# A convolution and a column recurrence on one core: the first stage moves into the blocks' buffers, and the matrices in memory get 112 rows

## The chip, the cores and the metric

The kernel runs on one core of a Trainium2 chip. A core has five engines with a queue of instructions each: PE (TensorE, matrix products; its weight loads are listed apart as PEld), ACT (ScalarE), DVE (VectorE), POOL (GpSimd) and SP (SyncE, which here only issues transfers). Sixteen DMA engines move data between the chip's memory (HBM) and the core's buffers (SBUF, 128 partitions); PE writes to PSUM. Engines wait for each other and for transfers by semaphores. The metric is the device time of one execution in microseconds (us). Before the change three runs took 5189.91, 5190.26 and 5219.42 us; the median is 5190.26.

## The reference

The input `x` has 4 images of 64 channels, 256 x 256 pixels, float32. Two layers are computed, each on a group norm of its input and added to it:

```python
x = x + _L0_conv_ref(_gn(x), ...)   # layer 0
x = x + _L1_conv_ref(_gn(x), ...)   # layer 1

def _L0_conv_ref(x, w1, w_dw, w_out, ln_w, ln_b):
    hidden = einsum('bchw,oc->bohw', x, w1)            # 64 -> 384 channels, pointwise
    hidden = depthwise 3x3 convolution of hidden, padding SAME
    q, k, v = split(hidden, 3, axis=1)                 # 128 channels each
    out = irfft2(rfft2(patches8x8(q)) * rfft2(patches8x8(k)))
    out = layer norm of out over the channels
    return einsum('bchw,oc->bohw', v * out, w_out)     # 128 -> 64 channels
```

`_gn` is a group norm with 32 groups of 2 channels, so every image needs its mean and variance before anything of it can be convolved. Layer 1 is a gated recurrent cell (`_gru_cell`) that walks over the 256 columns of the image; a column takes the column before it, shifted by -1, 0 and +1 rows, as its state.

## The kernel before, in words

The program has three parts in order of time.

**The first stage** (lines 211 to 274) does two things at once. It builds the matrices of layer 0: a depthwise 3x3 convolution followed by the transform of an 8x8 patch is, per channel, one product of the 10x10 window (`HALO = 100` values) with a 100 x 64 matrix. `bt` (the constants of the nine taps) and `wd` (the weights) are multiplied on PE in 32 steps into PSUM (`banks`), ACT copies each step into `ts`, and three transfers on POOL's queue (`keep_matrices`) write `ts` to memory as `t_all`, of shape [3, 100, 8, 1024]: kind 0 for q, 1 for k, 2 for v, 100 rows of 8 groups of 16 channels. Beside this, `seen_piece` loads image 0 in 16 pieces of 1 MB through SP into five rotating buffers (`xc`), and DVE takes their statistics (`bn_stats`); after the last piece `norm_of_pieces` (line 83) turns them into the scale and shift of image 0 (`sc0`). The windows of the first block, `xq`, four transfers of 800 KB, come on POOL's queue behind the three `t_all` writes. The stage has pools of its own (`xa`, `sta`, `bps`), which are given back at its end.

**Layer 0** (lines 276 to 709) handles 32 blocks of 32 image rows one after the other. `normalize` applies the group norm to `xq`. Then PE makes `h`, the pointwise product, for one third of the channels at a time (three chunks of 16 units; `pointwise`), and after each chunk multiplies `h` by the matrices: `transform` for q and k (`circular` takes their product and `inverse` transforms it back into `z`), `values` for v. The layer norm (`layer_norm`), the gate and the projection of a block run beside the next block's products. The matrices do not stay in SBUF: `fetch` brings them anew for each block, 24 transfers of 16 channels, each [100 rows, 1024 values], 400 KB, through SP into four rotating tiles `t` (line 326). A fetch is issued four matrices ahead, and waits until PE has finished with the matrix that was in its tile. `wk` holds the work space of q and k, `seen` the piece of the next image whose statistics are taken in passing (`look`, `count`), on POOL's queue.

**Layer 1** (lines 716 to 900) goes over the 256 columns.

The order on each engine is that in which the program is written: every instruction goes through `InOrder`, which keeps it. Waits are derived from the tiles that instructions read and write. SP's queue is used by the pieces, the constants, the fetches and the residual loads (`residual`); POOL's by `t_all`, `xq`, `look` and the stores of layer 0's result (`leave`); ACT's by the taps and weights. An instruction that waits holds up everything behind it on its queue.

Of the kernel before, what the change touches and what calls it, by code (L numbers as in the profile page):

```python
# [9 lines left out]
F32 = mybir.dt.float32  # L10
# [6 lines left out]
HID = 6 * C  # L17
# [7 lines left out]

NBLK = B * W // 32
HALO = 100
NJ = 64
NP = 2 * NJ

# [52 lines left out]
def norm_of_pieces(nc, st, t, psum, eps, sc):  # L83

    m_all, d, total, mean = t[:, 256:264], t[:, 264:272], t[:, 272:273], t[:, 273:275]
    nc.vector.tensor_copy(m_all, st[:, :, 0])
    nc.vector.tensor_reduce(total, m_all, mybir.AxisListType.X, ALU.add)
    yield  # L90
    pm = psum()
    for i in range(2):
        nc.tensor.matmul(pm[:, i : i + 1], lhsT=t[:, P * i : P * i + P], rhs=total, start=True, stop=True)
    nc.vector.tensor_copy(mean, pm)
    nc.vector.tensor_tensor(d, m_all, mean[:, 0:1].to_broadcast([P, 8]), ALU.subtract)
    nc.vector.tensor_tensor(d, d, d, ALU.mult)
    nc.vector.tensor_tensor(d, d, st[:, :, 1], ALU.add)
    nc.vector.tensor_reduce(total, d, mybir.AxisListType.X, ALU.add)
    yield
    pv = psum()[:, 0:1]  # L100
    nc.tensor.matmul(pv, lhsT=t[:, P : 2 * P], rhs=total, start=True, stop=True)
    nc.scalar.activation(sc[:, 1:2], pv, AF.Sqrt, bias=eps, scale=1.0)
    nc.vector.reciprocal(sc[:, 1:2], sc[:, 1:2])
    nc.vector.scalar_tensor_tensor(sc[:, 0:1], mean[:, 1:2], -1.0, sc[:, 1:2], ALU.mult, ALU.mult)
    yield
# [57 lines left out]
def tile_conv_then_gru(  # L163
# [21 lines left out]
    x1 = dram.tile([B, C, W, H], F32, tag="x1", name="x1")  # L185


    t_all = dram.tile([3, HALO, 8, 16 * NS], F32, tag="t_all", name="t_all")


    layer0 = ExitStack()
    xp = layer0.enter_context(tc.tile_pool(name="xp", bufs=4))
    xq = {}

    def load(n, jq):

        t = xp.tile([P, 16, HALO], F32, tag="xq", name=f"xq_{n}_{jq}")
        nc.gpsimd.dma_start(t, xh[n, :, 16 * jq : 16 * jq + 16, :])
        xq[n, jq] = t

    def piece(of, b, i, w, n):

        w0 = i * (W // 16) + w
        return of[b].rearrange("c (a w) h -> (c a) w h", a=2)[:, w0 : w0 + n, :].rearrange("p w h -> p (w h)")
# [3 lines left out]
    sc0 = const.tile([P, B, 2], F32, tag="sc0", name="sc0")  # L208
    st0 = const.tile([P, 8, 2], F32, tag="st0", name="st0")
    bn0 = const.tile([P, 8, 6], F32, tag="bn0", name="bn0")  # L210
    with tc.tile_pool(name="xa", bufs=5) as xa, tc.tile_pool(name="sta", bufs=1) as sta, tc.tile_pool(
        name="bps", bufs=1, space=PSUM
    ) as bps:
        bt = sta.tile([P, 32, HALO], F32, tag="bt", name="bt")
        wd = sta.tile([P, HID], F32, tag="wd", name="wd")
        for i in range(4):
            nc.scalar.dma_start(wd[32 * i : 32 * i + 9], w_dw)
            nc.scalar.dma_start(bt[32 * i : 32 * i + 9], taps[i])
        eps = const.tile([P, 1], F32, tag="eps", name="eps")
        nc.gpsimd.memset(eps, EPS)  # L220
        ts = sta.tile([HALO, 3 * P, NS], F32, tag="ts", name="ts")
        banks = bps.tile([P, 8, 512], F32, tag="b", name="psb")

        def keep_matrices(i):
            nc.gpsimd.dma_start(
                t_all[i].rearrange("p n k -> p (n k)"),
                ts[:, i * P : (i + 1) * P].rearrange("p c k -> p (c k)"),
            )

        for i in range(32):  # L230
            kind, s = i // 16, i % 16
            c0, num = 2 * P * kind, 2 * P - P * kind
            ps = banks[0:HALO, 4 * (i % 2) : 4 * (i % 2) + 4, 0:num]
            for k in range(4):
                at = slice(32 * k, 32 * k + 9)
                nc.tensor.matmul(
                    ps[:, k],
                    lhsT=bt[at, i, :],
                    rhs=wd[at, c0 : c0 + num],
                    start=True,  # L240
                    stop=True,
                    tile_position=(32 * k, 0),
                )
            nc.scalar.copy(ts[:, c0 : c0 + num, 4 * s : 4 * s + 4], ps.rearrange("p s c -> p c s"))
            if i == 15:
                keep_matrices(0)
                keep_matrices(1)
        keep_matrices(2)
        for jq in range(4):
            load(0, jq)  # L250
        def seen_piece(i):
            xc = xa.tile([P, 2048], F32, tag="xc", name=f"xc_{i}")
            nc.sync.dma_start(xc, piece(x, 0, i // 2, i % 2 * 8, 8))
            for k in range(4):
                nc.vector.bn_stats(bn0[:, i % 2 * 4 + k, :], xc[:, 512 * k : 512 * k + 512])
            if i % 2:
                nc.vector.bn_aggr(st0[:, i // 2, :], bn0)

        for i in range(6):
            seen_piece(i)  # L260
        avg = sta.tile([P, 512], F32, tag="avg", name="avg")
        nc.sync.dma_start(avg[:, 0 : 2 * P].rearrange("p (a q) -> p a q", a=2), sums)
        w1_sb = const.tile([P, HID], F32, tag="w1", name="w1_sb")
        nc.sync.dma_start(w1_sb, w1.rearrange("a c o -> (a c) o"))
        g_sb = const.tile([P, 2, 2, NS], F32, tag="g", name="g_sb")
        nc.sync.dma_start(g_sb, g12.rearrange("a s r n p -> (a s) r n p"))
        wo_sb = const.tile([P, 4, C], F32, tag="wo", name="wo_sb")
        nc.sync.dma_start(wo_sb, w_out.rearrange("a f b c -> (a f) b c"))
        ln_sb = const.tile([P, 2, 4], F32, tag="ln", name="ln_sb")
        nc.sync.dma_start(ln_sb, ln.rearrange("a f n b -> (a f) n b"))  # L270
        for i in range(6, 16):
            seen_piece(i)
        for _ in norm_of_pieces(nc, st0, avg, lambda: banks[:, 0:2, 0], eps, sc0[:, 0]):
            pass
    st1 = const.tile([P, NBLK, 2], F32, tag="st1", name="st1")
    with layer0 as s:
        big = s.enter_context(tc.tile_pool(name="big", bufs=1))
# [8 lines left out]
            place[0] = (at + banks) % 8  # L286
            return ring[:, at % 8 : at % 8 + banks]

        h = big.tile([HALO, P, NP], F32, tag="h", name="h")
        z = big.tile([P, NJ, E], F32, tag="z", name="z")  # L290
        v = big.tile([P, NJ, E], F32, tag="v", name="v")
        wk = big.tile([P, 7, 1024], F32, tag="wk", name="wk")
        lnst = big.tile([P, 512], F32, tag="lnst", name="lnst")
        seen = big.tile([P, 1024], F32, tag="seen", name="seen")
        moments = big.tile([P, 2, NJ], F32, tag="moments", name="moments")
        def normalize(n, jq):

            t, b, at = xq[n, jq], n // 8, n % 8
            flat = t.rearrange("p j k -> p (j k)")
            shift, rstd = sc0[:, b, 0:1], sc0[:, b, 1:2]  # L300
            if jq == 3:
                nc.vector.tensor_scalar(flat, flat, rstd, shift, ALU.mult, ALU.add)
            else:
                nc.scalar.activation(flat, flat, AF.Identity, bias=shift, scale=rstd)
            grid = t.rearrange("p j (r c) -> p j r c", c=10)
            if jq % 2 == 0:
                nc.gpsimd.memset(grid[:, 0, :, 0:1], 0.0)
            else:
                nc.gpsimd.memset(grid[:, 15, :, 9:10], 0.0)
            if at == 0 and jq < 2:  # L310
                nc.gpsimd.memset(grid[0:C, :, 0, :], 0.0)
            if at == 7 and jq >= 2:
                nc.gpsimd.memset(grid[C:P, :, 9, :], 0.0)
# [8 lines left out]
        def fetch(count):  # L322
            while len(streamed) < min(count, NBLK * 24):
                m, r = divmod(len(streamed), 24)
                t = tp.tile([P, 16, NS], F32, tag="t", name=f"t_{m}_{r}")
                nc.sync.dma_start(t[0:HALO].rearrange("p c k -> p (c k)"), t_all[order[r][0], :, order[r][1]])
                streamed.append(t)
                matrices[m, order[r]] = t

# [270 lines left out]
        def go(steps=1):  # L600
            for _ in range(steps):
                if norm:
                    next(norm, None)

        for n in range(NBLK + 1):
# [14 lines left out]
            for unit in range(16):  # L620
                if unit < 14:
                    pointwise(n, 0, unit, unit in (3, 9) if norm else unit % 2)
                elif unit == 14:
                    last_two = [unit_of(n, 0, unit, False)]
                else:
                    last_two.append(unit_of(n, 0, unit, False))
                    for span in ((0, 16), (16, P)):
                        for copy in last_two:
                            copy(*span)
                if unit in (0, 3, 6, 9, 12):  # L630
                    go()

            def beside_first(sp):
                if n and sp < 3:
# [326 lines left out]
```

## Time and profile before

One execution was profiled: its own time is 5200.96 us, and its span, from the first to the last instruction, is 5199.2 us.

| what | value |
|---|---|
| median of three runs | 5190.26 us |
| profiled execution, span | 5200.96 us, 5199.2 us |
| first stage, up to the first pointwise matmul | 102.8 us |
| layer 0, 32 blocks | from there to about 3760 us |
| busy PE, DVE, ACT, POOL | 4911.1, 4038.0, 3348.7, 1724.5 us |
| fetches of matrices | 768 of 400 KB |
| writes of the matrices | 3 of 3200 KB, landing after 19.8, 31.5 and 34.7 us |
| moved by DMA in all | 784.55 MB, mean 151 GB/s |

How to read the answers of the profile: a row of the timeline has the start (us), the busy time of a run of like instructions (us), the engine, the line in the kernel, the operation, output and input, and in brackets how long the engine had been idle and what ended that. Nearly all instructions have line 157, that of `InOrder`, so tiles tell them apart. The row of a group has its count, then the sum and the mean (ns) of its busy time, then the idle time just before its instructions, by releaser. "issue" is idle time for which the profile shows no releaser. DMA share is the mean share of the time in which the sixteen DMA engines had a packet in hand.

### The profile page before, as it was taken

Reading aid. Unit: us, or ns where it says so; the run is one execution under the profiler, and the core shown is the slowest. Engines: PE = TensorE matmul, PEld = TensorE weight load, DVE = VectorE, ACT = ScalarE, POOL = GpSimd, SP = SyncE. Lnnn points to the kernel's source line nnn. Section 1 sums busy time; section 2 is a strip of 40 time slices with the busy share of each in tenths; the row PEclk is TensorE's granted clock in tenths of the full one; section 3 lists DMA queues with packets and bytes.
Section 4 is the critical chain, followed back from the end, with each engine's and each line's share of the span. In section 5 each row is a group of like instructions: output and inputs, shape, how many; then the busy total and the mean of one; then the engine's idle time right before and its main releaser. Section 6 shows DMA issues by size and latency. Waiting matters only on the chain.

```text
span 5199.2 us, 275863 instructions
## 1 busy us (share of the span) xinstructions
PE 4911.1 (94%) x127092; PEld 4202.2 (81%) x127092; DVE 4038.0 (78%) x7000; ACT 3348.7 (64%) x4253; POOL 1724.5 (33%) x1723
## 2 busy tenths in 40 slices
PE   4999999999999999999999999999789999999999
PEld 3887888788888888888887888888578888888888
DVE  4678888877888887788887777878667777777777
ACT  3666667666666766666666666667466666666665
POOL 0233333333333333333333323223333333333333
PEclk9999999999999999999999999999899999999999
DMA  7566665666666666666656656655443333333332
GB/s 266 148 171 178 185 180 166 168 175 169 171 188 173 171 170 175 172 178 180 186 160 162 151 155 164 168 159 151 111 123 99 100 98 99 100 100 100 97 100 71
DMA packets 421174, 784.55 MB, mean 151 GB/s; under 512 B 32604, under 2 KB 295552, under 8 KB 417632
## 3 DMA queue, kind: packets, MB, share of 16 engines
q1 hardware_dynamic: 366464, 533.76, 38.1%
q0 software_dynamic: 53264, 232.55, 15.3%
q8 instruction: 997, 16.33, 1.4%
q14 instruction: 161, 1.32, 0.1%
q10 hardware_dynamic: 288, 0.58, 0.0%
HBM read 622.72 MB, written 144.05 MB: 147 GB/s over the span
## 4 chain that ended last, share of the span: by engine, by line
PE 78%; DVE 7%; issue 5%; ACT 5%; DMA 4%; POOL 1%; ACTq 0%; POOLq 0%; SPq 0%; DVEq 0%
PE psring L157 57%; PE pshz L157 7%; PE pshr L157 6%; PE psni L157 5%; PE pshn L157 3%; DMA t<-t_all 2%; ACT z L157 2%; DVE n L157 2%; ACT v L157 1%; DVE wk L157 1%; ACT xq L157 1%; DVE st L157 1%; DVE g L157 1%; DVE z L157 1%; DMA wk<-in_sums 1%
## 5 line engine op out<-in xcount | busy, mean ns | idle before, releaser
L157 PEld LDWEIGHTS psring<-h,t 100*32 100x32 f32 x49152 | 1383.5, 119 | 249.1 <-issue 195.7
L157 PE MATMUL psring<-h,t 100*32 100x128 f32 x49152 | 1464.3, 257 | 96.7 <-issue 59.0
L157 PEld LDWEIGHTS psring<-w_sb,xq 64*100 64x100 f32 x24576 | 1372.6, 164 | 123.1 <-issue 89.7
L157 PE MATMUL psring<-w_sb,xq 64*100 64x128 f32 x24576 | 1430.4, 273 | 34.2 <-issue 21.6
L157 ACT COPY h<-psring 100x1024 f32<-100x1024 f32 (+2 forms) x1371 | 1234.1, 988 | 336.8 <-PE psring L157 335.9
L157 DVE TENSOR_TENSOR wk<-psring,wk 128x1024 f32<-128x1024 f32 (+1 forms) x768 | 759.5, 1037 | 461.5 <-PE psring L157 320.2
L157 POOL TENSOR_TENSOR v<-v,z 128x2048 f32<-128x2048 f32 x128 | 582.7, 4557 | 658.6 <-DVE wk L157 603.0
L157 DVE TENSOR_TENSOR z<-z,moments 128x2048 f32<-128x2048 f32 x256 | 578.0, 2279 | 2.3
L157 POOL TENSOR_TENSOR wk<-wk 128x1024 f32<-128x1024 f32 x128 | 303.4, 2371 | 618.7 <-DVE wk L157 596.6
L157 POOL TENSOR_TENSOR raw<-raw,st 128x512 f32<-128x512 f32 x256 | 303.1, 1184 | 530.6 <-DVE st L157 471.5
L157 ACT COPY z<-psring 128x2048 f32<-128x2048 f32 x128 | 238.9, 1866 | 348.8 <-PE psring L157 248.2
L157 PE MATMUL pshr<-st,wi 64*64 64x144 f32 (+7 forms) x12240 | 429.7, 269 | 6.7 <-DVE st L157 6.7
L157 DVE COPY h<-psring 100x1024 f32<-100x1024 f32 x229 | 277.5, 1214 | 198.7 <-PE psring L157 192.7
L157 PE MATMUL psni<-st,wi 64*64 64x144 f32 (+7 forms) x12240 | 428.6, 269 | 1.3 <-issue 1.3
L157 PE MATMUL pshz<-st,wi 64*64 64x144 f32 (+7 forms) x12240 | 428.8, 269 | 0.1
L157 ACT ACTIVATE z<-pshz,b_rz 128x288 f32<-128x288 f32 (+7 forms) x510 | 242.0, 475 | 281.3 <-PE pshz L157 275.8
L157 ACT COPY wk<-psring 128x1024 f32<-128x1024 f32 x256 | 259.5, 1014 | 249.5 <-PE psring L157 214.4
L157 DVE BATCH_NORM_STATS2 lnst<-z 128x6 f32<-128x128 f32 x2048 | 416.8, 282 | 0.0
L157 ACT COPY v<-psring 128x2048 f32<-128x2048 f32 (+1 forms) x160 | 243.3, 1521 | 251.0 <-PE psring L157 251.0
L157 PEld LDWEIGHTS pshr<-st,wi 64*64 64x64 f32 x12240 | 370.0, 133 | 41.1 <-DVE st L157 9.8
L157 PEld LDWEIGHTS psni<-st,wi 64*64 64x64 f32 x12240 | 369.7, 133 | 31.3 <-issue 0.7
L157 PE MATMUL psring<-wk,g_sb 32*64 32x512 f32 x6144 | 382.1, 600 | 9.2 <-issue 5.9
(96 smaller groups left out, 6170.2 us busy)
## 6 DMA issues: line engine op xcount, KB each, us to landing
t<-t_all SPq DMA_DIRECT2D x768, 400.0 KB
xq<-in_xh POOLq DMA_DIRECT2D x128, 800.0 KB, 6.1
wk<-in_x SPq DMA_DIRECT2D x256, 256.0 KB
x<-wk POOLq DMA_DIRECT2D x256, 256.0 KB, 5.4
seen<-in_x POOLq DMA_DIRECT2D x96, 512.0 KB, 7.6
raw<-x SPq DMA_DIRECT2D x128, 256.0 KB
raw<-x SPq DMA_DIRECT2D x256, 128.0 KB
out<-raw SPq DMA_DIRECT2D x128, 256.0 KB
```

Of the source, the lines that this page charges most:

```text
L157: return self.tc.keep_in_program_order(got(*args, **kwargs))
```

## The change

The first stage no longer has buffers of its own. `h`, `z`, `v` and `wk` of layer 0 are allocated first, and the stage borrows them: the image pieces, `bt`, `wd` and `avg` lie in `h` (`hx`), the matrices of kind 0 in `wk`, of kind 1 in `z`, of kind 2 in `v`; `seen` becomes an eighth slice of `wk`. The matrices go to memory later: kinds 0 and 1 on SP's queue after the last image piece, in three transfers, kind 2 on POOL's queue in the first block, after the sixteenth unit of its first chunk. `xq` of block 0 comes on SP's queue, between the pieces, and the weights `wd` on POOL's. ACT copies a step of kinds 0 and 1 in two instructions instead of one, and applies a Sqrt to one column before the norm. The stage computes with `ring`, the PSUM tile of layer 0.

In memory `t_all` has `ROWS = 112` rows instead of 100, and every fetch brings 112. The last twelve are zeros (cleared by one memset on DVE and two on POOL, from row 96 on); PE reads 100 as before.

```diff
 HALO = 100
+ROWS = 112
...
-    t_all = dram.tile([3, HALO, 8, 16 * NS], F32, tag="t_all", name="t_all")
+    t_all = dram.tile([3, ROWS, 8, 16 * NS], F32, tag="t_all", name="t_all")
...
-    def load(n, jq):
+    def load(n, jq, queue=nc.gpsimd):
...
-        nc.gpsimd.dma_start(t, xh[n, :, 16 * jq : 16 * jq + 16, :])
+        queue.dma_start(t, xh[n, :, 16 * jq : 16 * jq + 16, :])
...
+        hx = big.tile([P, P * NP], F32, tag="h", name="h")
+        h = hx[0:HALO].rearrange("p (c n) -> p c n", n=NP)
...
+        wk = big.tile([P, 8, 1024], F32, tag="wk", name="wk")
+        seen = wk[:, 7]
...
+        bt = hx[:, 10240:13440].rearrange("p (i k) -> p i k", k=HALO)
+        wd = hx[:, 13440 : 13440 + HID]
+        avg = hx[:, 13824 : 13824 + 512]
+        ts = (
+            wk[0:ROWS].rearrange("p a (c k) -> p (a c) k", k=NS),
+            z[0:ROWS].rearrange("p n e -> p (n e)").rearrange("p (c k) -> p c k", k=NS),
+            v[0:ROWS].rearrange("p n e -> p (n e)").rearrange("p (c k) -> p c k", k=NS),
+        )
         for i in range(4):
-            nc.scalar.dma_start(wd[32 * i : 32 * i + 9], w_dw)
             nc.scalar.dma_start(bt[32 * i : 32 * i + 9], taps[i])
+            nc.gpsimd.dma_start(wd[32 * i : 32 * i + 9], w_dw)
...
+        nc.vector.memset(wk[96:ROWS], 0.0)
+        for t in (z, v):
+            nc.gpsimd.memset(t[96:ROWS], 0.0)
+
+        def keep_matrices(queue, i, k0, k1):
+            queue.dma_start(
+                t_all[i, :, k0:k1].rearrange("p n k -> p (n k)"),
+                ts[i][:, 16 * k0 : 16 * k1].rearrange("p c k -> p (c k)"),
             )
...
-            nc.scalar.copy(ts[:, c0 : c0 + num, 4 * s : 4 * s + 4], ps.rearrange("p s c -> p c s"))
-            if i == 15:
-                keep_matrices(0)
-                keep_matrices(1)
-        keep_matrices(2)
-        for jq in range(4):
-            load(0, jq)
+            for part in range(2 - kind):
+                nc.scalar.copy(
+                    ts[2 * kind + part][0:HALO, :, 4 * s : 4 * s + 4],
+                    ps[:, :, P * part : P * part + P].rearrange("p s c -> p c s"),
+                )
+
+        for i in range(32):
+            matrices_of(i)
+        nc.scalar.activation(moments[:, 0, 0:1], eps, AF.Sqrt, bias=eps, scale=1.0)
+
         def seen_piece(i):
-            xc = xa.tile([P, 2048], F32, tag="xc", name=f"xc_{i}")
+            xc = hx[:, 2048 * (i % 5) : 2048 * (i % 5) + 2048]
...
-        for i in range(6):
+        for i in range(10):
             seen_piece(i)
+            if i in (4, 6, 8):
+                load(0, i // 2 - 2, nc.sync)
...
-        for i in range(6, 16):
+        for i in range(10, 16):
             seen_piece(i)
-        for _ in norm_of_pieces(nc, st0, avg, lambda: banks[:, 0:2, 0], eps, sc0[:, 0]):
+            if i == 10:
+                load(0, 3, nc.sync)
+        for i, k0, k1 in ((0, 0, 8), (1, 0, 4), (1, 4, 8)):
+            keep_matrices(nc.sync, i, k0, k1)
+        for _ in norm_of_pieces(nc, st0, avg, lambda: ring[:, 0:2, 0], eps, sc0[:, 0]):
             pass
...
-                nc.sync.dma_start(t[0:HALO].rearrange("p c k -> p (c k)"), t_all[order[r][0], :, order[r][1]])
+                nc.sync.dma_start(t[0:ROWS].rearrange("p c k -> p (c k)"), t_all[order[r][0], :, order[r][1]])
...
                 if unit in (0, 3, 6, 9, 12):
                     go()
+                if n == 0 and unit == 15:
+                    keep_matrices(nc.gpsimd, 2, 0, 8)
```

More of the change, by code (lines that the diff above doesn't have):

```diff
@@ L210, in tile_conv_then_gru @@
     bn0 = const.tile([P, 8, 6], F32, tag="bn0", name="bn0")
[L211 to L216, printed above, removed]
-            nc.scalar.dma_start(wd[32 * i : 32 * i + 9], w_dw)
[L218 to L243, printed above, removed]
-            nc.scalar.copy(ts[:, c0 : c0 + num, 4 * s : 4 * s + 4], ps.rearrange("p s c -> p c s"))
-            if i == 15:
-                keep_matrices(0)
-                keep_matrices(1)
-        keep_matrices(2)
-        for jq in range(4):
-            load(0, jq)
-        def seen_piece(i):
-            xc = xa.tile([P, 2048], F32, tag="xc", name=f"xc_{i}")
[L253 to L257, printed above, removed]
-        for i in range(6):
[L260 to L270, printed above, removed]
-        for i in range(6, 16):
-            seen_piece(i)
-        for _ in norm_of_pieces(nc, st0, avg, lambda: banks[:, 0:2, 0], eps, sc0[:, 0]):
-            pass
@@ L275, in tile_conv_then_gru @@
+    st1 = const.tile([P, NBLK, 2], F32, tag="st1", name="st1")
     st1 = const.tile([P, NBLK, 2], F32, tag="st1", name="st1")
@@ L287, in psum @@
             return ring[:, at % 8 : at % 8 + banks]
-        h = big.tile([HALO, P, NP], F32, tag="h", name="h")
+        hx = big.tile([P, P * NP], F32, tag="h", name="h")
+        h = hx[0:HALO].rearrange("p (c n) -> p c n", n=NP)
         z = big.tile([P, NJ, E], F32, tag="z", name="z")
         v = big.tile([P, NJ, E], F32, tag="v", name="v")
-        wk = big.tile([P, 7, 1024], F32, tag="wk", name="wk")
+        wk = big.tile([P, 8, 1024], F32, tag="wk", name="wk")
+        seen = wk[:, 7]
@@ L293, in tile_conv_then_gru @@
         lnst = big.tile([P, 512], F32, tag="lnst", name="lnst")
-        seen = big.tile([P, 1024], F32, tag="seen", name="seen")
         moments = big.tile([P, 2, NJ], F32, tag="moments", name="moments")
+        bt = hx[:, 10240:13440].rearrange("p (i k) -> p i k", k=HALO)
[6 more added lines that the diff above has]
+        )
@@ new lines, in tile_conv_then_gru @@
+        for i in range(4):
+            nc.scalar.dma_start(bt[32 * i : 32 * i + 9], taps[i])
+            nc.gpsimd.dma_start(wd[32 * i : 32 * i + 9], w_dw)
+        eps = const.tile([P, 1], F32, tag="eps", name="eps")
+        nc.gpsimd.memset(eps, EPS)
+        nc.vector.memset(wk[96:ROWS], 0.0)
[6 more added lines that the diff above has]
+            )
@@ new lines, in matrices_of @@
+        def matrices_of(i):
+            kind, s = i // 16, i % 16
+            c0, num = 2 * P * kind, 2 * P - P * kind
+            ps = ring[0:HALO, 4 * (i % 2) : 4 * (i % 2) + 4, 0:num]
+            for k in range(4):
+                at = slice(32 * k, 32 * k + 9)
+                nc.tensor.matmul(
+                    ps[:, k],
+                    lhsT=bt[at, i, :],
+                    rhs=wd[at, c0 : c0 + num],
+                    start=True,
+                    stop=True,
+                    tile_position=(32 * k, 0),
+                )
+            for part in range(2 - kind):
+                nc.scalar.copy(
+                    ts[2 * kind + part][0:HALO, :, 4 * s : 4 * s + 4],
+                    ps[:, :, P * part : P * part + P].rearrange("p s c -> p c s"),
+                )
@@ new lines, in tile_conv_then_gru, with seen_piece @@
+        for i in range(32):
+            matrices_of(i)
+        nc.scalar.activation(moments[:, 0, 0:1], eps, AF.Sqrt, bias=eps, scale=1.0)
+        def seen_piece(i):
+            xc = hx[:, 2048 * (i % 5) : 2048 * (i % 5) + 2048]
+            nc.sync.dma_start(xc, piece(x, 0, i // 2, i % 2 * 8, 8))
+            for k in range(4):
+                nc.vector.bn_stats(bn0[:, i % 2 * 4 + k, :], xc[:, 512 * k : 512 * k + 512])
+            if i % 2:
+                nc.vector.bn_aggr(st0[:, i // 2, :], bn0)
@@ new lines, in tile_conv_then_gru @@
+        for i in range(10):
+            seen_piece(i)
+            if i in (4, 6, 8):
+                load(0, i // 2 - 2, nc.sync)
+        nc.sync.dma_start(avg[:, 0 : 2 * P].rearrange("p (a q) -> p a q", a=2), sums)
+        w1_sb = const.tile([P, HID], F32, tag="w1", name="w1_sb")
+        nc.sync.dma_start(w1_sb, w1.rearrange("a c o -> (a c) o"))
+        g_sb = const.tile([P, 2, 2, NS], F32, tag="g", name="g_sb")
+        nc.sync.dma_start(g_sb, g12.rearrange("a s r n p -> (a s) r n p"))
@@ new lines, in tile_conv_then_gru @@
+        wo_sb = const.tile([P, 4, C], F32, tag="wo", name="wo_sb")
+        nc.sync.dma_start(wo_sb, w_out.rearrange("a f b c -> (a f) b c"))
+        ln_sb = const.tile([P, 2, 4], F32, tag="ln", name="ln_sb")
+        nc.sync.dma_start(ln_sb, ln.rearrange("a f n b -> (a f) n b"))
+        for i in range(10, 16):
+            seen_piece(i)
+            if i == 10:
+                load(0, 3, nc.sync)
+        for i, k0, k1 in ((0, 0, 8), (1, 0, 4), (1, 4, 8)):
+            keep_matrices(nc.sync, i, k0, k1)
@@ L296, in normalize @@
+        for _ in norm_of_pieces(nc, st0, avg, lambda: ring[:, 0:2, 0], eps, sc0[:, 0]):
+            pass
         def normalize(n, jq):
```

## The prediction

> **What bounds the kernel now.** I read the page first, for who is busiest. PE has 94% of the span, and in the page's chain of work that ended last it holds 78%. So time is won only where PE stands still; everything else is cover.
>
> ```profile
> PE 4911.1 (94%) x127092; PEld 4202.2 (81%) x127092; DVE 4038.0 (78%) x7000; ACT 3348.7 (64%) x4253; POOL 1724.5 (33%) x1723
> ...
> q8 instruction: 997, 16.33, 1.4%
> ```
>
> The second line is the queue that brings the program itself: 997 packets for 16.33 MB, so 16 KB a packet. Over 275,863 instructions that is 59 bytes each; as some records can be missing I take 64, and 256 instructions a packet.
>
> Then I asked who made PE wait, longest first in total (us, times, longest):
>
> ```profile
> PE psring L157 <- issue: 87.9, 95, 3.1
> ...
> PE psring L157 <- DMA t<-t_all: 15.3, 27, 1.6
> ```
>
> "issue" means that nothing in the profile was waited for. I laid these gaps beside the trace's records of the instruction queue: 95 of the layer's gaps end within 0.35 us of the end of a 16 KB packet on it. So they are PE out of instructions. After such a landing the next packet starts 2.6 us later at the earliest and takes about 1.05 us, 3.7 us in all; and 256 instructions are 128 matmuls with their weight loads, which in the transforms (320 matmuls in 8.99 us) last 3.6 us. There PE eats its program as fast as it can arrive, so whatever delays a packet stops PE. Of the 87.9 us, 59.0 lie ahead of the matmuls that read the matrices (row of the groups: idle before, by releaser):
>
> ```profile
> L157 PE MATMUL psring<-h,t 100*32 100x128 f32 x49152 | 1464.3, 257 | 96.7 <-issue 59.0 <-DMA t<-t_all 14.4 <-ACT h L157 13.1
> ```
>
> Last, the first stage, which ends at 102.77 us. Its stretches of 10 us (busy us of PE, PEld, DVE, ACT, POOL; clock; DMA share; GB/s):
>
> ```profile
> 0.00:10.00 10.00, 1.14 (x2) 0.40 (x2) 2.47 (x4) 0.00 (x0) 0.30 (x5) 1.00 0.87 230
> 10.00:20.00 10.00, 2.32 (x8) 0.88 (x8) 5.32 (x9) 1.28 (x1) 0.00 (x0) 1.00 0.99 257
> 20.00:30.00 10.00, 9.10 (x66) 3.91 (x66) 8.06 (x14) 7.68 (x8) 0.00 (x0) 1.00 0.89 336
> 30.00:40.00 10.00, 8.98 (x80) 3.89 (x76) 7.55 (x13) 8.27 (x10) 0.38 (x1) 1.00 1.01 423
> 40.00:50.00 10.00, 8.94 (x116) 5.77 (x112) 7.67 (x14) 7.85 (x14) 0.91 (x2) 1.00 1.04 405
> 50.00:60.00 10.00, 0.38 (x8) 0.04 (x4) 1.33 (x4) 0.71 (x2) 2.70 (x5) 1.00 1.01 384
> 60.00:70.00 10.00, 0.00 (x0) 0.00 (x0) 1.79 (x4) 0.00 (x0) 0.00 (x0) 1.00 0.94 366
> 70.00:80.00 10.00, 0.00 (x0) 0.00 (x0) 2.84 (x5) 0.00 (x0) 0.00 (x0) 1.00 0.91 341
> 80.00:90.00 10.00, 0.00 (x0) 0.00 (x0) 2.47 (x4) 0.00 (x0) 0.00 (x0) 1.00 0.82 293
> ```
>
> From 50 us on all engines stand and the DMA runs full: the stage is as long as the bytes ahead of its last image piece. These rows hold 30.4 MB by 90 us. The page's DMA list gives what went: image pieces 16 x 1024 KB = 16.8 MB, xq 4 x 800 KB = 3.3, constants 1.1, and t_all 3 x 3200 KB = 9.8; together 31.0. The timeline shows the pieces held back behind t_all, then the end of the stage:
>
> ```profile
> 47.80 2.47 DVE L157 BATCH_NORM_STATS2 bn<-xc 128x6 f32<-128x512 f32 x4 [2.26 <-DMA xc<-in_x]
> ...
> 92.40 2.47 DVE L157 BATCH_NORM_STATS2 bn<-xc 128x6 f32<-128x512 f32 x4 [3.09 <-DMA xc<-in_x]
> ...
> 98.56 1.28 ACT L157 ACT_TABLE_LOAD   x1 [47.52 <-PE psb L157]
> ...
> 102.77 16.56 PEld L157 LDWEIGHTS psring<-w_sb,xq 64*100 64x100 f32 x256 [4.39 <-POOL xq L157]
> ```
>
> **The first stage.** *Moved:* t_all's writes now stand behind the last piece on SP's queue. Ahead of the piece are 16.8 + 3.3 + 1.1 = 21.2 MB. By the rows 16.5 MB have moved at 50 us; the other 4.7 at 384 GB/s take 12.2, so it lands at 62. From the last landing to the first matmul it is 102.77 - 92.40 = 10.4 us; the Sqrt table, now loaded early, takes 1.28 off that: 71. I add 2 us for pieces waiting for one of five buffers, as now: 73, **30 us earlier**.
>
> *Added, hidden:* ACT's 16 copies of 1024 elements (1.01 us) become 32 of 512 (0.57 us by the row of that size), 2 us more; they end near 53 instead of 51, before 62. DVE clears 16x8192 of wk first: by its TENSOR_SCALAR of 1600 elements (1.11 us) 5.7 us, by its COPY of 1024 (1.23 us) 9.8; then 16 pieces of 2.84 us end by 56, before 62. POOL clears z and v: two memsets of xq (10 and 160 elements, 0.12 and 0.24 us) give 6.6 us each, the 2048-element multiply (4.56 us) 18; z is ready by 10 to 21, v by 17 to 40, first written by ACT at about 21 and 42. With that cover gone each of these would push ACT by its own length, and the piece at 62 still ends later.
>
> *Late next:* t_all. wk and z hold 2 x 3.67 MB on SP; at 375 GB/s (the rows of 50 to 70) they end at 82, the first four matrices (1.8 MB) at 87. They are needed 17 us after the first matmul, at 90. But POOL adds an image look (0.5 MB, waiting for wk's write, with v's write queued behind it; POOL's next work, the first crossed add, is 27 us behind the first matmul now) and v's 3.67 MB from about 78, and between 50 and 70 POOL's queue visibly took more than SP's. If all 4.2 MB go first, the matrices come at 98, 8 us late; if none, not late. I take 4: **-26 us**. Ends: -30, and -10 if HBM takes the writes at about half pace (then 16 more are lost). z's first write, 14 us after the transforms begin, and v's, 80 after, come behind the writes that read them.
>
> **The fetches.** 768 fetches now carry 112 rows. A packet of a row takes 159 ns in most records. Where only matrices move, the records show ten packets in flight at 614 of 1,178 sampled moments, over eleven at 9: 100 rows use ten DMA engines of sixteen. The 128-row pieces fill sixteen (share 1.01 above), the 9-row taps go as nine packets each. I infer that rows are split evenly over the most engines that divide them: 112 = 16 x 7. Ends: ten engines as for 100 rows, sixteen as for 128; I take sixteen. Then an engine gets 7 packets, 1.1 us, in place of 10, 1.6 us. In a transform a matrix is used up in 1.87 us, so ten engines are 85% full with t alone, sixteen 60%. The 37.7 MB more (768 x 49 KB) take 2.6% of sixteen engines over the layer, mean DMA share 0.62: no cost while it stays below full. SP issues the same 768.
>
> The Trainium skill, page "DMA: Bandwidth & Descriptors", section "Why a DMA increments its semaphore by 16 and not by 1", states the same split and names 100 partitions as ten engines; by it 112 are sixteen. If it were ten, both terms below would be nothing.
>
> What waits on them: the chain of waits runs over a fetch some two dozen times, as here (start, us, what), issue to landing 5.4 to 6.9 us:
>
> ```profile
> 123.68 5.61 DMA t<-t_all
> 129.29 0.14 issue
> 129.42 31.94 PE psring L157 x782
> ```
>
> Four buffers leave a fetch three matrices' time, 3 x 1.87 = 5.6 us. With 0.5 us less work and no standing queue it fits: of 15.3 us I take **-13** (ends 0 and -15).
>
> **The program's own packets** share these engines. In stretches where nothing but t had moved in the 4 us before, the records show 52 gaps (47 us) ahead of h,t and 7 (5 us) ahead of g_sb. After a landing the next packet starts at 2.6 to 2.8 us in about a third of the cases and at 3 to 8 in the rest, also beside t alone, as if some packets met t's queue and some did not. Sixteen less full engines should halve these 52 us: **-25**. Ends: -52, and a loss (below). The 22 us ahead of the pointwise matmuls come beside xq loads and stay.
>
> **Sum:** -26 - 13 - 25 = -64 us. The profiled execution took 5200.96 us (span 5199.2 and 1.8 around it): 5137. It lies 10.7 above the median of the three runs, 5190.26, so the median becomes **5126 us**, 1.2% faster. 1%, 52 us, is about what a measurement of this kernel can tell from no change.
>
> **Rivals.**
> - *The packets of the program do not care* (0.20). For it: 2.6 us of their 3.7 is a fixed delay. Against: long delays occur beside t alone. Then 5190 - 39 = **5151**.
> - A rule in the Trainium skill would make it so: "Runtime: NRT & Kernel Launch", section "Instruction fetch mechanics", calls the cost of crossing a 16 KiB block mostly hidden; the 95 gaps that end on such a packet speak against it here.
> - *The change does not do what it says* (0.10): 112 rows stay on few engines, and only the stage gains: **5164**.
> - *The stage gives back its gain* (0.11): t_all lands late, -10 in place of -26: **5142**.
> - *Slower* (0.07): the program's packets lie on the six engines that t leaves free today, and t now covers all sixteen. The h,t matmuls are 98,304 instructions, 384 packets, of which some 62 end a gap today, 0.94 us each. If a third of the other 322 get one, that is +101; with -26 and -13, +62: **5252**. It decides for "slower by 1%" from about 97 new gaps (91 us). Against: the 52 gaps beside t alone, which free engines would not have.
>
> **Numbers.** The forecast has 0.52. Its own spread is about 5100 to 5150, below 5138 in three of four; with a third of the late stage and a fifth of the first rival that makes 0.47 for faster by over 1%, 0.07 for slower, 0.46 between. The range goes from 5098 (-30, -15, -47) to 5172 (past the stage-only case, with some of its loss) and leaves out the slower rival and the far ends.
>
> **What would show it.** The first pointwise matmul near 73 us and the first transform by 90 to 95; the chain no longer over t; PE's wait for t under 3 us; more packets of t in flight than ten; "issue" on psring near 60 us. Wrong if "issue" grows, if the transforms of the first image wait past 98, or if the last image piece is not at 62.

## The result, and the profile after

The changed kernel took 5150.57 us (median of 6 runs, 5141.58 to 5159.27), the kernel before on the same chip 5199.66 (6 runs, 5189.91 to 5219.42): a ratio of 0.9902, 95% interval 0.9881 to 0.9923, so 1.0% faster. The forecast was 5126 of 5190, a ratio of 0.9876. The profiled execution of after took 5159.27 us, its span is 5157.5, 41.7 less than before.

The page of after: busy time, the instruction queue, and who holds the chain that ended last.

```profile
PE 4895.8 (95%) x127092; PEld 4200.1 (81%) x127092; DVE 4043.5 (78%) x7001; ACT 3349.0 (65%) x4270; POOL 1738.5 (34%) x1723
...
q8 instruction: 997, 16.33, 1.4%
...
PE 82%; DVE 6%; ACT 5%; issue 4%; POOL 1%; DMA 0%; ACTq 0%; POOLq 0%; DVEq 0%; SPq 0%
```

The same row of the chain before:

```profile
PE 78%; DVE 7%; issue 5%; ACT 5%; DMA 4%; POOL 1%; ACTq 0%; POOLq 0%; SPq 0%; DVEq 0%
```

DMA had 4% of that chain before and has none now: it no longer runs over the fetches. Who made PE wait in after (us, times, longest), then the groups of the matmuls that read the matrices and of the pointwise ones, and last the pointwise group before:

```profile
PE psring L158 <- issue: 128.8, 133, 17.8
```

```profile
L158 PE MATMUL psring<-h,t 100*32 100x128 f32 x49152 | 1464.8, 257 | 112.9 <-issue 91.2 <-ACT h L158 14.7 <-ACT xq L158 0.3
L158 PE MATMUL psring<-w_sb,xq 64*100 64x128 f32 x24576 | 1415.9, 272 | 22.5 <-issue 9.1 <-DVE wk L158 4.4 <-ACT z L158 4.2
```

```profile
L157 PE MATMUL psring<-w_sb,xq 64*100 64x128 f32 x24576 | 1430.4, 273 | 34.2 <-issue 21.6 <-POOL xq L157 4.3 <-ACT z L157 4.2
```

PE has no wait for t left; it was 15.3 us. But "issue" has not shrunk. Of its 128.8 us, 17.8 are the norm's matmul, which stood under another tile before, and 8.6 belong to block 0, below; 102 are left, against 87.9. It moved, too: ahead of the pointwise matmuls from 21.6 to 9.1 us, ahead of h,t from 59.0 to 83. A second execution of the changed kernel (e10, below) has the same move (5.2 and 69 us), though only 80 us in all.

The first stage in stretches (columns as in the prediction), and its end and the first transforms on the timeline of PE:

```profile
30.00:40.00 10.00, 8.98 (x88) 4.63 (x88) 8.30 (x15) 8.32 (x16) 0.00 (x0) 1.00 1.01 415
40.00:50.00 10.00, 5.97 (x72) 3.79 (x72) 5.40 (x10) 7.29 (x13) 0.00 (x0) 1.00 1.03 408
50.00:60.00 10.00, 0.00 (x0) 0.00 (x0) 9.29 (x17) 0.00 (x0) 0.00 (x0) 1.00 1.05 437
...
90.00:100.00 10.00, 1.43 (x44) 1.19 (x39) 0.00 (x0) 1.01 (x1) 0.00 (x0) 0.76 0.57 208
100.00:110.00 10.00, 10.00 (x276) 10.00 (x272) 4.53 (x4) 1.47 (x2) 0.00 (x0) 0.73 0.45 125
```

```profile
70.28 16.52 PE L158 MATMUL psring<-w_sb,xq 64*100 64x128 f32 x256 [3.02 <-POOL xq L158]
88.77 1.96 PE L158 MATMUL psring<-h,t 100*32 100x128 f32 x64 [1.98 <-ACT h L158]
99.30 11.88 PE L158 MATMUL psring<-h,t 100*32 100x128 f32 x320 [8.57 <-issue]
```

The pointwise matmuls begin at 70.3 us instead of 102.8. Then the second matrix arrives 8.6 us late. The profile names no releaser for this stop, but the fetch of the second matrix lands at 99.21 in its records, and no packet of the program ends between 89.5 and 101.6. The stop costs twice: the clock is at half from 95.1 to 105.4, and five matrices (320 matmuls) take 11.9 us where before 320 took 8.99. The list of transfers says what was in the way (KB, us from issue to landing): z's two writes, issued at 49, have landed by 85, and v's write, issued on POOL's queue at 74, moves beside the fetches until 99.

```profile
t<-t_all SPq DMA_DIRECT2D x768, 448.0 KB, 4.7
...
t_all<-wk SPq DMA_DIRECT2D x1, 3584.0 KB, 20.8
t_all<-z SPq DMA_DIRECT2D x2, 1792.0 KB, 34.9
t_all<-v POOLq DMA_DIRECT2D x1, 3584.0 KB, 24.8
```

To see where time goes I use a mark that every block has, close to the end of `h`'s first chunk: the start of the last row of ACT's copies of 128 elements on the timeline (in block 0, of the row ahead of it, 0.9 us earlier). Blocks 1 to 31 are from the second mark to the last (us). The last column counts the "issue" gaps in them ahead of the two groups of matmuls that run while mostly t alone moves, h,t and g_sb:

```
                      block 0   block 1   block 31   blocks 1-31   gaps ahead of h,t and g_sb ("issue")
before                 118.72    225.79    3625.96     3400.2        60, 52.3 us
after                   85.96    206.62    3585.85     3379.2       102, 82.7 us
after again (e10)       89.70    204.88    3560.34     3355.5         96, 65.9 us
rows only  (e1)        116.21    222.04    3594.52     3372.5       112, 78.7 us
stage only (e2)         85.29    215.26    3598.82     3383.6        63, 58.7 us
late v     (e3)         85.90    200.28    3568.15     3367.9       106, 78.6 us
no refetch (e4)         88.04    207.48    3486.93     3279.4         1,  0.2 us
```

So the stage is 33 us shorter at its first mark, 14 of these are lost in block 0, and the 31 blocks give 21. Such a row is one execution: the changed kernel profiled again (e10) had 3355.5 for its blocks, 24 us less. Verdicts therefore go by the repeated runs.

### The profile page after: what moved, and what is told of

Its sections match the earlier page's. It is cut to its first block, busy times and chain, and to the rows that moved or that the text cites. A ratio compares the mean times of both kernels' runs of the same rounds, so it can differ in the third digit from the quotient of the medians.

```text
span 5157.5 us, 275884 instructions
## 1 busy us (share of the span) xinstructions
PE 4895.8 (95%) x127092; PEld 4200.1 (81%) x127092; DVE 4043.5 (78%) x7001; ACT 3349.0 (65%) x4270; POOL 1738.5 (34%) x1723
## 4 chain that ended last, share of the span: by engine, by line
PE 82%; DVE 6%; ACT 5%; issue 4%; POOL 1%; DMA 0%; ACTq 0%; POOLq 0%; DVEq 0%; SPq 0%
PE psring L158 61%; PE pshz L158 7%; PE pshr L158 6%; PE psni L158 5%; PE pshn L158 3%; ACT z L158 2%; DVE n L158 2%; ACT v L158 1%; DVE st L158 1%; DVE g L158 1%; ACT xq L158 1%; DVE wk L158 1%; DVE z L158 0%; POOL v L158 0%; DVE lnst L158 0%
## 5 line engine op out<-in xcount | busy, mean ns | idle before, releaser
L158 PE MATMUL psring<-h,t 100*32 100x128 f32 x49152 | 1464.8, 257 | 112.9 <-issue 91.2
L158 PE MATMUL psring<-w_sb,xq 64*100 64x128 f32 x24576 | 1415.9, 272 | 22.5 <-issue 9.1
L158 ACT COPY z<-psring 128x2048 f32<-128x2048 f32 (+1 forms) x144 | 248.5, 1726 | 351.8 <-PE psring L158 255.1
L158 ACT COPY wk<-psring 128x1024 f32<-128x1024 f32 (+1 forms) x272 | 269.1, 989 | 283.6 <-PE psring L158 247.3
L158 DVE COPY h<-psring 100x1024 f32<-100x1024 f32 (+1 forms) x230 | 278.0, 1209 | 196.9 <-PE psring L158 196.8
L158 ACT COPY v<-psring 128x2048 f32<-128x2048 f32 (+2 forms) x176 | 252.5, 1436 | 251.3 <-PE psring L158 251.0
```

What stands on the lines that cost most here:

```text
L158: return self.tc.keep_in_program_order(got(*args, **kwargs))
```

## The experiments

**e1: the rows alone.** The kernel before, with

```diff
-    t_all = dram.tile([3, HALO, 8, 16 * NS], ...)
+    t_all = dram.tile([3, ROWS, 8, 16 * NS], ...)
...
-        ts = sta.tile([HALO, 3 * P, NS], ...)
+        ts = sta.tile([ROWS, 3 * P, NS], ...)      # rows 96 to 111 cleared on POOL
...
-    nc.sync.dma_start(t[0:HALO]...
+    nc.sync.dma_start(t[0:ROWS]...
```

> The kernel before with 112 rows in memory and in every fetch, first stage as before (three memsets on POOL clear the twelve rows). Theory A, the rows act by themselves: PE's wait for t falls from 15 us to under 3 and blocks 1 to 31 get 21 us shorter, as in the changed kernel; time ratio to before 0.996. Theory B, the layer's gain came with the new place of the buffers and the shifted phases of the transfers: ratio 1.000 within 0.001, t waits stay above 10 us.

Measured: 5162.35 us, ratio 0.9925 (0.9906 to 0.9943), 39 us less. The t waits fell to 1.1 us. Theory A holds in kind; the gain is larger than the 21 us I had read off the changed kernel's blocks. It is also most of what the whole change gains: the interval overlaps that of the changed kernel (0.9881 to 0.9923), so that the stage adds to the rows is not shown by these two.

**e2: the stage alone.** The changed kernel with `ROWS = HALO` and without the memsets.

> The changed kernel with 100 rows again (no memsets): the first stage alone. Theory A: blocks 1 to 31 take as long as in the kernel before (3400 us from the end of the first chunk of block 1 to that of block 31), the gain is the 20 us of the stage, ratio 0.996; t waits come back to about 15 us. Theory B: the blocks keep their 21 us, ratio 0.992.

Measured: 5196.77 us (12 runs), ratio 0.9993 (0.9975 to 1.0012): no gain at all, which neither theory had. The first mark is 33 us earlier, as in the changed kernel, and t waits return (8.1 us in the blocks). But block 0 takes 130 us, where before took 107 and the changed kernel 121. (The profiled execution is the fastest of its twelve, so only block 0 is read from it.) The timeline of e2, PE, shows the place:

```profile
70.14 15.97 PE L158 MATMUL psring<-w_sb,xq 64*100 64x128 f32 x256 [2.96 <-POOL xq L158]
109.95 8.30 PE L158 MATMUL psring<-h,t 100*32 100x128 f32 x212 [23.84 <-DMA t<-t_all]
```

PE waits 23.8 us for the first matrix. The writes of `t_all` by SP carry 100 rows too, and in the records ten of their packets are in flight, sixteen with 112 rows. A 32 KB packet of wk's write lasts 1.44 us on average, and the write takes 18.7 us from its first packet to its last; with 112 rows it is 1.23 and 11.5. z's writes end at 99.7 instead of 84.2. v's write ends later still, at 108.1, and PE goes on 1.8 us later; in the changed kernel it goes on 1.0 us after the end of v's write, at 98.3. How much of the 23.8 us is due to which write was not tried apart. The rows thus pay twice, and with 100 of them the stage does not pay. The clock may have a part in it: the mean granted clock of e2's twelve runs is 0.9877, that of the 17 runs of before beside them 0.9905. I estimate that at 15 us at most, a thousandth of the span for each thousandth, and less where the half clock fell into a wait.

**e3: v later.** The changed kernel, with

```diff
-                if n == 0 and unit == 15:
-                    keep_matrices(nc.gpsimd, 2, 0, 8)
...
             circular(n, 0, beside_first)
+            if n == 0:
+                keep_matrices(nc.gpsimd, 2, 0, 8)
```

> The changed kernel with the write of v's matrices moved from the first chunk of block 0 to behind its first circular (v is needed only in the third chunk). Theory 1, v's 3.67 MB on POOL's queue hold up the first fetches: the transform's second matrix comes at about 90 us instead of 99.3, PE's clock stays up, 9 to 13 us are won against the changed kernel, ratio to before 0.988. Theory 2, the writes of wk and z alone fill the time: the second matrix still comes after 96 us and at most 3 us are won.

Measured: 5140.99 us, ratio 0.9883 (0.9865 to 0.9902). PE on its timeline:

```profile
88.37 9.55 PE L158 MATMUL psring<-h,t 100*32 100x128 f32 x338 [1.64 <-DMA t<-t_all]
98.58 1.51 PE L158 MATMUL psring<-h,t 100*32 100x128 f32 x46 [0.66 <-issue]
...
112.82 5.43 PE L158 MATMUL psring<-w_sb,xq 64*100 64x128 f32 x68 [3.91 <-issue]
```

The transforms run through from 88.4, and block 1's mark comes at 200.3 instead of 206.6. Theory 1 holds by the place; the 10 us lie inside the spread of the two ratios. Of the stop's cost a part comes back: v's packets now move from 104.5 to 116.6, and beside them the pointwise matmuls stand still for 3.9 us, with no releaser in the profile.

**e4: no fetch after block 0.** Blocks 1 to 31 use the four matrices left in the tiles.

```diff
+                if m:
+                    t = streamed[20 + r % 4]
+                else:
                     t = tp.tile(...); nc.sync.dma_start(...)
```

> The changed kernel without any fetch after block 0: blocks 1 to 31 use the four matrices that were left in the tiles (so what is computed from them is left out). Theory C, as predicted: the gaps of PE ahead of h,t that end on program packets come from t's traffic: the 91 us of issue ahead of h,t fall under 25 and blocks 1 to 31 get 60 us or more shorter. Theory D, the packets' own 3.7 us against 3.6 us of work is the limit whatever else moves: issue ahead of h,t stays above 60 us.

Measured: 5057.0 us in one run, 94 us less than the changed kernel's median. The row of the transforms:

```profile
L158 PE MATMUL psring<-h,t 100*32 100x128 f32 x49152 | 1434.5, 257 | 35.4 <-ACT h L158 12.8 <-issue 7.3 <-DMA t<-t_all 5.3
```

"issue" ahead of h,t falls from 91.2 to 7.3 us, in blocks 1 to 31 from 72.6 to 0.2, and the blocks are 100 us shorter (76 against those of e10). Theory D falls. Without t's traffic the program arrives in time even in the transforms; beside it, PE runs dry about a hundred times.

**e5: the second half of kind 1 later too.** e3, with `fetch(4)` before `keep_matrices(nc.sync, 1, 4, 8)`.

> The kernel with v's write moved behind the first circular, and now the write of the second half of the matrices of kind 1 behind the first four fetches too. If the writes ahead of the first fetches still cost time, the first transform comes right behind the first chunk (within 0.5 us) and the ratio to before falls from 0.988 to 0.987; if not, it stays at 0.988, and the first fetches wait for something else.

Measured: 5134.76 us, ratio 0.9882 (0.9858 to 0.9907). The first transform now follows the first chunk after 0.4 us, as hoped, and the ratio is that of e3: the 1.3 us won are below what these runs can tell.

**e6, e7, e8: other numbers of rows.** The changed kernel with `ROWS = 104`, `128` and `101`.

> The changed kernel with 104 rows. Theory E, the program's packets meet t's queue wherever a fetch runs, and a fetch runs on the most engines that divide its rows: 104 rows run on thirteen engines with 8 packets each; in blocks 1 to 31 the gaps ahead of h,t and g_sb that end on program packets number between 60 (100 rows, ten engines) and 102 (112 rows, sixteen): about 78; t waits lie between 14 us and 0. Theory F, only the load matters (bytes): gaps as with 112 rows or fewer, about 90 to 100, and no t wait.

> The changed kernel with 128 rows: sixteen engines as with 112, 8 packets each in place of 7, 14% more bytes a fetch. If what counts is how many engines a fetch runs on, no t waits and about 100 gaps on program packets, time within 0.2% of the changed kernel (ratio 0.990); if bytes count, longer gaps (mean above 0.95 us) and 20 us or more lost (ratio above 0.994).

> The changed kernel with 101 rows, a prime. If rows are split evenly over the most engines that divide them, a fetch runs on one engine: 101 packets of 159 ns or more, 16 us for a matrix that is used up in 1.87 us, 768 x 16 = 12.3 ms for the layer, 13 to 15 ms in all. If rows are dealt out to ten or more engines whatever their number, the time is within 1% of the kernel before.

Measured: 101 rows 14,898 us; 104 rows 5197.47 us, ratio 1.0011 (0.9995 to 1.0027); 128 rows 5126.94 us, ratio 0.9867 (0.9842 to 0.9892). With 101 rows PE on this row waits 7096 us for t:

```profile
L158 PE MATMUL psring<-h,t 100*32 100x128 f32 x49152 | 2528.3, 357 | 7634.8 <-DMA t<-t_all 7096.3 <-DVE wk L158 513.6 <-ACT h L158 12.8
```

The packets' records, where only t moves (most common number in flight; all t packets' mean and median ns):

```
rows   in flight   mean   median   gaps ahead of h,t and g_sb, blocks 1-31
100       10        214     160      60, mean 0.87 us
101        1        163     159      -
104       13        239     204      89, mean 0.92 us
112     15-16       234     166     102, mean 0.81 us
128       16        211     159      88, mean 0.73 us
```

The number of engines is settled: 1, 10, 13 and 16, the largest number up to sixteen that divides the rows, as I had inferred from 100, 128 and 9. The Trainium skill, page "DMA: Bandwidth & Descriptors", section "Why a DMA increments its semaphore by 16 and not by 1", states this rule, and the trace agrees.

The rest did not come as either theory had it. 104 rows have 89 gaps, nearer F's 90 to 100 than E's 78, and still wait for t (4.5 us in the blocks); their stage loses 24 us in block 0 as e2's did (23.8 us waiting for t), and nothing is won in all. Thirteen packets of wk's write are in flight here, yet it takes 19.9 us, as a packet lasts 1.83 us on average: the number of engines alone does not give the price of a write either. 128 rows, with 14% more bytes than 112, are not slower but 0.35% faster by the medians of the ratios; the intervals just overlap. Their packets are shorter on average, 211 ns against 226 to 236 in the five executions with 112 rows (after, e1, e3, e5, e10), and the gaps fewer, 88 against 96 to 112. A gap is not shorter than in all of these (0.73 us against 0.69 to 0.81):

```profile
L158 PE MATMUL psring<-h,t 100*32 100x128 f32 x49152 | 1461.7, 257 | 90.3 <-issue 68.8 <-ACT h L158 12.7 <-DMA t<-t_all 1.1
```

Why a packet of a 128-row fetch is quicker than one of 112 or 104 was not tried further, and stays open.

**e9, e10: what helped, together.** e5 with `ROWS = 128`, beside the changed kernel on the same chip.

> Both steps that helped, together: v's write and the second half of kind 1 behind the first fetches, and 128 rows. If they add, as their places in time suggest (block 0 and blocks 1 to 31): 10 us from block 0 and 20 us from the blocks against the changed kernel, ratio to before 0.984 (within 0.982 to 0.987). If one hides the other: 0.987.

> The changed kernel itself on the same chip, as the measure for the run beside it: ratio to before 0.990 (0.988 to 0.992).

Measured: 5110.36 us, ratio 0.9860 (0.9842 to 0.9877), against 5126.00, ratio 0.9898 (0.9884 to 0.9913). The intervals lie apart: e9 beats both kernels, by 1.4% the one before and by 0.3% the changed one. The ratio fell by 0.0038, where the two steps alone had 0.0020 (e5) and 0.0035 (e7). The interval reaches into the range given for steps that add and holds the 0.987 of one hiding the other, so this does not tell which.

## Why the prediction was right or wrong

The time came out inside the range, the sign and the size of the gain were right (1.0% against 1.2%), and one of its three terms was wrong. That the sum held is in part luck. The two terms for the rows come to 38 us and e1 measured 39 for the rows alone, but one of the two had the wrong sign; gains that no term stood for made up for it. Of the prediction's own signs of being wrong one is met in the profile of after, "issue" grew (in e10 ahead of h,t and g_sb alone), and one nearly: the first transforms began at 88.8, but their second matrix came at 99.3, past 98.

- **The first stage, -26.** Right in its steps: first pointwise matmul at 70.3 (forecast 73), because the last piece landed at 60.7 (forecast 62) once `t_all` was behind it, and the table load was gone from the chain. "Late next: t_all" was right as well, mis-sized: I took 4 us between 0 and 8, and the 8 of the far end, matrices at 98, was close to what came. Measured were some 10 us of waiting (2.0 ahead of the first matrix, of which a normal start has 0.4, and 8.6 ahead of the second), and 2.9 us of halved clock behind the wait, which the step did not have. Block 1's mark is 19 us earlier. By the repeated runs the stage adds some 12 us to the rows alone (0.9902 against 0.9925), in overlapping intervals. e3 shows that v's write on POOL's queue was the cause, not slow writes of wk and z. What I missed altogether is e2: with 100 rows this stage gains nothing. I had counted the writes' bytes at 375 GB/s and not asked on how many engines they run, ten as the records show.
- **The waits for t, -13.** Right: 15.3 us before, none after, 1.1 with the rows alone.
- **The program's packets, -25.** Wrong, and this is the step that failed: "Sixteen less full engines should halve these 52 us". They became 82.7 us in the blocks (65.9 in the second execution, e10). The premise was right, and more so than I thought: without t the gaps vanish (e4). The tie to the program's packets holds too, with a lag that the prediction misread: in the records of before all 95 gaps end 1.1 to 1.7 us behind the end of such a packet, not within 0.35 us of it. And the shortest time from packet to packet is 3.35 us, not 3.7, a little less than the 3.6 us of work that a packet brings; so there is a small reserve, as e4 shows. The consequence was not right. The gaps grew in number, 60 to 102 (96 in e10), and shrank in length, 0.87 to 0.81 us (0.69). A factor of 1.6 to 1.7 is close to the 16/10 that follows if every packet that was safe on an engine without t now meets t; that is the mechanism of my slower rival at a smaller price. e6 does not fit it well (89 gaps at thirteen engines), so the count by engines is argued, not shown; that spreading did not reduce the sum is shown by the five executions with 112 rows (65.9 to 82.7 us) against the two with 100 (52.3 and, in e2, 58.7).
- **What made up for it.** The profiled span fell by 42 us: 19 up to block 1's mark, 21 in the blocks, 2 behind them. In the blocks PE's idle time hardly changed, 118.0 us before and 115.2 after: the waits for t fell by 14 and the gaps ahead of h,t and g_sb grew by 30, but ahead of the pointwise matmuls "issue" fell from 21.6 to 8.7 us and the waits for the norm's constants from 8.0 to 2.4. These two lie outside my terms. The rest of the 21 us is PE's busy time, 16 us less, and with the long gaps went halved clock: the trace's clock records have 47.8 us of half clock between 230 and 3540 us before, 27.3 after, 17.1 with the rows alone. Each of the ten stretches before began within 1.3 us of the end of a gap of 1.7 us or more, none at the many short ones. 20.5 us fewer at half clock are worth 10. The other 6 us of busy time I can't place; the second execution of the changed kernel is 24 us shorter in its blocks than the first.
- **The rivals.** "The stage gives back its gain", at 5142, was the nearest to what block 0 did. "The packets do not care" came nearest in time, 5151 against 5150.57, and is wrong in its mechanism: e4 shows that they care a great deal.

The Trainium skill, page "Runtime: NRT & Kernel Launch", section "Instruction fetch mechanics", calls the cost of crossing a 16 KiB block of the program mostly hidden. That holds in e4 and in layer 1 (0.6 us of issue in after); beside a steady stream of fetches the trace disagrees, with about 100 gaps of 0.7 to 0.8 us.

## What to carry to other kernels

- The number of rows of a transfer decides on how many engines it runs, and this holds for the writes on SP's queue as for the reads (10, 13, 16 and 1 packets in flight with 100, 104, 112 and 101 rows): choose rows that sixteen divides, and pay the padding. Here 12% more bytes in each fetch gave 0.75% (e1). With 28% more the changed kernel was 1.3% under the one before instead of 1.0%, in intervals that just overlap.
- A shorter first stage is worth what the next stage can take: look up what the moved transfers collide with, on every queue. Work that nobody needs for 70 us (v's matrices, written from 74 on and first fetched at 144) should not be issued in front of what is needed in 15.
- Where PE runs many short matmuls, its own program is a stream with a deadline. A gap of "issue" that ends with a packet of the instruction queue is traffic's work; what removes it is less traffic: without the fetches (e4, one run) the kernel took some 90 us less.

## What the runs showed of the hardware that was not expected

- One engine for 101 rows: the same kernel, 2.9 times as long.
- Sixteen engines at 112 rows give longer packets (mean 226 to 236 ns in five executions) than at 128 (211, and 209 in e9), and thirteen at 104 longer ones still (239, median 204 against 160 with 100 rows).
- PE's clock was halved for 3.4 or 6.8 us at single gaps of 1.7 to 3.1 us (before: at ten of the 14 gaps of 1.7 us or more, and at all eight over 2 us), and for 10.2 us from inside the 8.6 us stop in block 0. In after it was halved at some gaps of 1.5 us and not at others of 1.9. The Trainium skill, page "TensorE: Matmul & The Clock Gate", section "HAM oscillation — how this bites in real kernels", puts the limit for such gaps at about 3.4 us; here shorter ones often sufficed.
